# Five attention layers on one core: weights and context loaded before a branch, and the maxima of 16-head cross-attention split over two items

## The chip, the cores and the metric

The kernel runs on one core of a Trainium2 chip. The metric is the device time of one execution in microseconds (us). Before the change three runs took 2417.28, 2418.72 and 2425.54 us, a median of 2418.72.

A core has engines that run side by side, each through its own list of instructions, in order: PE (TensorE, matrix multiplication, and PEld, its loads of the stationary operand), DVE (VectorE), ACT (ScalarE), POOL (GpSimd) and SP (SyncE, here only the issuer of DMAs). An instruction that waits holds up all that stand behind it on its engine. Matrix results land in PSUM, from where DVE or ACT take them to SBUF ("evacuate" them); here PSUM is divided into a pool p1 of four buffers and a pool pb of two.

## The reference

Four sequences (batches) x of 1024 tokens by 256 channels, and a context of 77 rows by 256 for each batch, go through these layers, with residuals:

```python
# layer 0: pre-norm; self-attention with a mask, cross-attention, feed-forward
h = layernorm(x); x = x + mha16(h, h, h, mask)
h = layernorm(x); x = x + mha16(h, ctx, ctx)
h = layernorm(x); x = x + relu(h @ w1 + b1) @ w2
# layer 1: three times 4-head attention with relu on Q, K, V; first to ctx, then to itself
#   enc = norm(softmax(Q K' / 8, masked rows) V + q); enc += leaky_relu(enc @ Wff + bff)
# layer 2 (l2): 16-head cross-attention to ctx, out projection, residual, layernorm
# layer 3 (l3): 16-head cross-attention to ctx, no projection, residual, layernorm
```

All of it is in float32. The mask of these inputs lets the tokens of the first self-attention see only a few (at most 32) keys, all among the last ones. The kernel finds that out on the chip, and branches on it.

## The kernel before

*Items.* The work is cut into items, one for each batch and layer: four of the masked self-attention with few keys (SelfFew), four of layer 0's cross-attention (Cross16 with the layer named ca, whose feed-forward is part of the item's end), four of layer 1's first attention (Cross4), eight of its self-attention (Self4), four Cross16 of l2 and four Cross16 of l3. In time they take roughly 30 to 240 us (SelfFew), 240 to 605 (ca and its feed-forward), 605 to 1900 (layer 1), 1900 to 2180 (l2) and 2180 to 2417 (l3).

*Stages of an item.* An item has three lists of work. `start()` prepares it: norm, turning tokens to channels, queries, maxima. `attend()` yields units, 8 of them for Cross16: four groups of heads (g) for each half of the tokens (c = 0, 1; 512 tokens each). `end()` finishes it: projection, residual, norm, feed-forward. `Pipe.run` walks through the items' units, and at each unit a `Pump` (L84) issues steps between the unit's scores and its weighted sum. A pump draws on two lists: the first has `item.more()` and the `start()` of the next item, the second the `end()` of the item before. A step has a cost; the pump issues so many that the share of the costs done keeps up with the share of the units done, choosing the list that is further behind. A step's `lag` keeps its successor in the list back until that much cost has been issued, and a `test` keeps it back until something has happened. At the last unit everything left is issued. `until(test)` issues steps of the first list, without regard to shares, until the test holds: `attend()` calls it before the first unit of each half, where the half's shift must be there. This fixes the order on PE, which is issued as written; the order on DVE, ACT and POOL is made by a scheduler from the same program.

*A unit of Cross16.* `scores` (L335): the eight matmuls L346 and L352 make scores pb of four heads, with the shift added by the four of L352, and two exponentials on ACT (L356) make PT. `weighted` (L359): the matmuls L365 make po, evacuated to OT by ACT or DVE. A unit later `normal` (L372) transposes OT (L377) and divides by the sum (r, L380, and att, L382, on DVE).

*Maxima and shift.* So that the exponentials stay in range, each query's score is shifted by its maximum over the keys. `maxima(e, t)` (L265) makes all scores of eight heads for 128 tokens with two matmuls into two p1 buffers (pa, L270), and two DVE reductions take the maxima (mx, L275). For a half there are eight maxima (e = 0, 1 and four t). `shift(c)` (L296) follows: four DVE operations (L304 to L307) split the negated maxima into three bfloat16 parts (m), PE transposes them (pm, L310), and the result is evacuated to SH, which L352 adds. In `Cross16.start` (L213) the order is, for c = 0 and then c = 1: norm, two turns (L252), two queries (L260), eight maxima, shift. So both halves' maxima are issued in the attention of the item before. SelfFew does the same with its own maxima (L914, L921), four for each half.

*Norms.* At the end of an item of l2 and l3, `stats` and `norm` (L428, L432) run on DVE, with one small POOL operation between (pw, L1509): batch norm statistics (L1500, L1501), then L1547 and L1550, x with weight and bias of the norm. For l2 and l3 the next layer's turns read x as it is; where a layer has a norm in front (ca, feed-forward, SelfFew) a normalised copy xn is made in a buffer with the tag F, of which there is one.

*The beginning.* `branch` (L1915) loads the mask (raw, 1 MB of bytes, two DMAs issued by ACT) and x[0] (1 MB, SP). `mask_kind` (L1754) casts the mask to bfloat16 in eight pieces (mk, four buffers; L1766 on DVE, L1768 on ACT), sums its columns on PE (L1770), and DVE derives from the sums which kind of mask it is (kind). `orders` (L1815) prepares constants, `few_keys` (L1793) the valid keys, `first_norm` (L1877) the norm of x[0], `context` (L1862) loads the context per batch (cx, 77 rows, four DMAs issued by POOL into two buffers), transposes it (L1870) and sums it (ctx_sums, L1872). Then the engines read kind and branch. Behind the branch `l0_weights` (L1889) issues the self-attention's weights on SP (wk, wv, wq, wo; wk and wq share a buffer wqk), and two small loads on POOL (bvc and row, L1897 and L1899); x[1] and x[2] follow on SP, and x[3] later, in the place of a buffer that the beginning used. `LayerFew.steps` (L796) has a step `close`: DVE copies Q's and K's weights without their padding into a buffer named room (L812). Keys (pk, L877) and queries (pp, L867) of SelfFew read them there.

Of the kernel before, what the change touches and what calls it, by code (L numbers as in the profile page):

```python
# [83 lines left out]
class Pump:  # L84
# [32 lines left out]
    def until(self, test):  # L117
        while not test():
            self.take(0)


class Pipe:
# [26 lines left out]
    def run(self, items):  # L149
        pump = Pump(self, 1, items[0].start(), [])  # L150
        pump.until(lambda: items[0].halves >= 1)
        left = pump.lists[0]
        before = None
        for a, b in zip(items, items[1:]):
            b.prev = a
        for i, item in enumerate(items):
            last = i + 1 == len(items)
            first = left + ([] if last else items[i + 1].start())
            second = (before.end() if before else []) + (item.end() if last else [])
            left = []  # L160
            idle = item.idle()
            self.pump = pump = Pump(self, item.units + idle, item.more() + first, second)
            for _ in range(idle):
                self.unit()
            for scores in item.attend():
                self.unit(scores, item.cost)
            before = item
        while self.due:
            pump.n = 0
            self.unit()  # L170
        pump.n = pump.units - 1
        pump()


class Item:
# [5 lines left out]
    def more(self):  # L181

        return []

# [4 lines left out]
    def __init__(self, net, layer, b):  # L189
        self.net, self.l, self.b = net, layer, b  # L190
        self.halves, self.ended = 0, 0
        self.prev, self.later_half = None, True

    def room(self):
# [10 lines left out]
class Cross16(Item):  # L205
# [7 lines left out]
    def start(self):  # L213
# [23 lines left out]
        def norm(c):  # L237
            if l.norm is None:
                self.xn = x[:, 4 * c : 4 * c + 4, :]
                return  # L240
            mv, rstd = self.mv, self.rstd
            self.xn = net.tile("F", [P, 4, C], name="xn")
            for i in range(4):
                t = 4 * c + i
                nc.vector.tensor_scalar(
                    self.xn[:, i, :], x[:, t, :], mv[:, t, 0:1], rstd[:, t : t + 1], ALU.subtract, ALU.mult
                )

        def turn(c, cc):
            pt = net.p1.tile([P, 512], F32, tag="p1", name="pt")  # L250
            for i in range(4):
                nc.tensor.transpose(pt[:, ts(i, P)], self.xn[:, i, ts(cc, P)], net.ident)  # L252
            at = None if l.norm is None else COL_LN + 4 * (l.norm - 1) + cc
            g, be = (None, None) if at is None else (net.cols[:, at : at + 1], net.cols[:, at + 2 : at + 3])
            net.evac(self.hT[:, cc, ts(c, 512)], pt, g, be)

        def query(e, c):
# [22 lines left out]
        step(0, new, lag=8 * ln)  # L280
        for c in range(2):
            step(0, norm, c, lag=3 * ln)
            step(0.5, turn, c, 0)
            step(0.5, turn, c, 1, lag=2)
            if c == 0:
                step(0, new_q, test=self.room)
            for e in range(2):
                step(1.8, query, e, c)
            for e in range(2):
                for i in range(4):  # L290
                    step(0.55, maxima, e, 4 * c + i, lag=3 if (e, i) == (1, 3) else 0)
            step(0.3, self.shift, c)
            step(0, self.have_half)
        return steps

    def shift(self, c):  # L296

        net, h = self.net, H16
        nc = net.nc
# [6 lines left out]
        nc.vector.tensor_copy(parts[1], left)  # L306
        nc.vector.tensor_tensor(parts[2], left, parts[1], ALU.subtract)  # L307
        pm = net.p1.tile([P, 512], BF16, tag="p1", name="pm")
        for i in range(4):
            nc.tensor.transpose(pm[:, ts(i, P)], m3[:, i, :], net.identb)  # L310
        net.evac(self.sh[:, c, :], pm)
# [219 lines left out]
class Feed:  # L531
# [15 lines left out]
    def steps(self, b):  # L547
# [10 lines left out]
        def norm(c):  # L558
            s["xn"] = net.tile("F", [P, 4, C], name="xn")
            for i in range(4):  # L560
                t = 4 * c + i
                nc.vector.tensor_scalar(
                    s["xn"][:, i, :], x[:, t, :], s["mv"][:, t, 0:1], s["rstd"][:, t : t + 1], ALU.subtract, ALU.mult
                )

        def turn(c, cc):
            pt = net.p1.tile([P, 512], F32, tag="p1", name="pt")
            for i in range(4):
                nc.tensor.transpose(pt[:, ts(i, P)], s["xn"][:, i, ts(cc, P)], net.ident)
            at = COL_LN + 8 + cc  # L570
            net.evac(s["hT"][:, cc, ts(c, 512)], pt, net.cols[:, at : at + 1], net.cols[:, at + 2 : at + 3])

        def hidden(q, f):
# [31 lines left out]
        for c in range(2):  # L605
            step(0, norm, c, lag=3)
            step(0.5, turn, c, 0)
# [26 lines left out]
class Self16(Cross16):  # L634
# [8 lines left out]
    def start(self):  # L643
# [19 lines left out]
        def norm(c):  # L663
            self.xn = net.tile("F", [P, 4, C], name="xn")
            net.normal(self.xn, x, self.mv, self.rstd, c)

        def turn(c, cc):
            net.turn_normal(self.hT, self.xn, 1, c, cc)

        def query(g, c):  # L670
# [51 lines left out]
        for c in self.cs:  # L722
            if b:
                step(0, norm, c, lag=3)
                step(0.5, turn, c, 0)
# [60 lines left out]
class LayerFew:  # L786
# [9 lines left out]
    def steps(self):  # L796
# [5 lines left out]
        def close():  # L802
# [7 lines left out]
            for kind in ("wk", "wq"):  # L810
# [3 lines left out]
                    self.w[kind].rearrange("p cc (h r) -> p (cc h) r", r=h.slot)[:, :, 0 : h.dh],  # L814
                )
            self.pick = part(256, BF16).rearrange("p (g n) -> p g n", g=G)
            net.nc.vector.tensor_copy(
# [10 lines left out]
class SelfFew(Cross16):  # L828
# [5 lines left out]
    def start(self):  # L834
# [22 lines left out]
        def norm(c):  # L857
            self.xn = net.tile("F", [P, 4, C], name="xn")
            net.normal(self.xn, x, self.mv, self.rstd, c)

        def turn(c, cc):
            net.turn_normal(self.hT, self.xn, 1, c, cc)

        def query(e, c):
# [59 lines left out]
        for c in self.cs:  # L924
            if b:
                step(0, norm, c, lag=3)
                step(0.5, turn, c, 0)
# [7 lines left out]
            for t in range(4 * c, 4 * c + 4):  # L935
                step(0.9, maxima, t, lag=3 if t % 4 == 3 else 0)
            step(0.3, self.shift, c)
# [514 lines left out]
class Net:  # L1452
    def __init__(self, ctx, tc, t):
        self.ctx, self.tc, self.nc, self.t = ctx, tc, tc.nc, t
        self.flip = 0

    def evac(self, out, src, scale=None, bias=None):
# [127 lines left out]
    def load_attention(self, name, has_wo, tag):  # L1587
        nc, t = self.nc, self.t
        got = {}
        kinds = [("wk", 512), ("wv", C), ("wq", 512)] + ([("wo", C)] if has_wo else [])  # L1590
        both = self.work.tile([P, 2, NC, 512], F32, tag=tag, name="wqk", bufs=self.TAGS[tag][1])
        for kind, width in kinds:
            w = both[:, int(kind == "wq")] if width == 512 else self.wpool.tile(
                [P, NC, width], F32, tag=kind, name=kind, bufs=2 if kind == "wo" else 1
# [159 lines left out]
    def mask_kind(self, pool, raw):  # L1754
# [8 lines left out]
        for i in range(NT):  # L1763
            m = pool.tile([P, S], BF16, tag="mk", name="mk", bufs=4)
            if i % 3 == 0:
                nc.vector.tensor_copy(m, raw[:, i, :])  # L1766
            else:
# [93 lines left out]

    def context(self):  # L1862

        nc = self.nc
        for b in range(NB):
            cx = self.small.tile([SC, C], F32, tag="cx", name="cx", bufs=2)
            nc.gpsimd.dma_start(out=cx, in_=self.t["ctx"][b])
            pt = self.p1.tile([P, NC, P], F32, tag="p1", name="pt")
            for cc in range(NC):
                nc.tensor.transpose(pt[:, cc, 0:SC], cx[:, ts(cc, P)], self.ident[:SC, :SC])  # L1870
            self.evac(self.ctxT[:, :, ts(b, SC)], pt[:, :, 0:SC])
            nc.vector.tensor_reduce(self.ctx_sums[:, b : b + 1], cx, AX.X, ALU.add)  # L1872

# [15 lines left out]
    def l0_weights(self, few):  # L1889
# [3 lines left out]
        nc, h = self.nc, H16  # L1893
        w = self.load_attention("sa", True, "B" if few else "E")
        rows = self.t["rows"][ROW["sa"], :]
# [19 lines left out]
    def branch(self, out):  # L1915
        nc, tc = self.nc, self.tc
        with tc.tile_pool(name="begin", bufs=1) as pool:
            raw = pool.tile([P, NT, S], U8, tag="rawk", name="rawk")
            for i in range(2):
# [3 lines left out]
                )  # L1923
            self.load_x(0)
            self.orders(pool)
            kind = self.mask_kind(pool, raw)
            self.few_keys(pool)
            self.first = self.first_norm(pool)
            self.context()

# [11 lines left out]
        with branch.Else():  # L1942
            with tc.If(asked(1) > 0) as general:
                with tc.tile_pool(name="work_g", bufs=1) as self.work:
                    w = self.l0_weights(False)
                    for b in range(1, NB):
                        self.load_x(b)
# [5 lines left out]
    def few_layer(self):  # L1953
        w = self.l0_weights(True)
        for b in range(1, NB - 1):
            self.load_x(b)
        return [(SelfFew, LayerFew(self, w))]

    def short_layer(self):
        w = self.l0_weights(False)  # L1960
        for b in range(1, NB - 1):
            self.load_x(b)
        return [(Self16, Layer16Self(self, w))]
# [191 lines left out]
```

## Time and profile before

| | |
|---|---|
| time of the three runs | 2417.28, 2418.72, 2425.54 us |
| time of the profiled execution | 2419.14 us |
| its span | 2417.3 us |
| mean granted TensorE clock | 0.951 of full speed |
| PE busy | 2196.4 us (91%) |
| DVE busy | 1582.1 us (65%) |
| ACT busy | 928.9 us (38%) |
| POOL busy | 382.3 us (16%) |
| maxima, L270 on PE | 167.2 us busy, 768 matmuls |
| maxima, L275 on DVE | 156.0 us busy, 384 operations |
| scores of Cross16, L346 | 114.5 us busy, 768 matmuls |
| weighted sums of Cross16, L365 | 136.8 us busy, 768 matmuls |
| HBM | 17.41 MB read, 4.19 MB written |

The profile is one execution. The page divides the span into 40 equal slices; each digit is an engine's busy share in tenths, and the line PEclk the clock that the TensorE was granted. In lines of the timeline the columns are the start in us, the time in us, the engine, the line of the kernel, the operation, the result and its operands, their shapes, how many such instructions in a row; in square brackets the idle time of the engine just before, and what ended it. In lines of the waits: an engine and the line that waited, what for, total us, number of times, the longest.

### The profile page before, as it was taken

How to read it: one execution, taken by the hardware profiler on the slowest of the kernel's cores; microseconds unless marked ns; L12 is line 12 of the kernel's file. 1: busy time of each engine (PE TensorE's matmuls, PEld its weight loads, DVE VectorE, ACT ScalarE, POOL GpSimd, SP SyncE). 2: the span in 40 equal slices, each digit the busy share in tenths (PEclk: the TensorE clock that was granted, in tenths of full speed). 3: DMA queues.
4: the chain of work that ended last, by engine and by line, in shares of the span. 5: the costliest groups of instructions: out<-in, count | busy, mean ns of one | idle time of the engine just before them, and what ended most of it. 6: DMA issues, size and time to landing. Idle time of an engine off the chain costs nothing. (4 is left out here: it accounts for less than half of the span.)

```text
span 2417.3 us, 31250 instructions
## 1 busy us (share of the span) xinstructions
PE 2196.4 (91%) x11035; PEld 1226.0 (51%) x11035; DVE 1582.1 (65%) x3170; ACT 928.9 (38%) x1828; POOL 382.3 (16%) x652
## 2 busy tenths in 40 slices
PE   4899999999999979999998999999999899898886
PEld 2556546666768645545443545444444444444331
DVE  5566655444233666888889688878887655655665
ACT  1222342222332545544444445444443343333333
POOL 2000000000000000333333233333232100000000
PEclk8999999999989989999999999999999898998888
DMA  4000010000000001677667576666785300000000
GB/s 128 18 1 16 5 35 1 1 7 5 7 5 3 1 5 34 149 160 151 144 144 159 120 149 146 148 148 146 154 156 111 70 5 1 5 1 1 27 18 28
DMA packets 148550, 158.01 MB, mean 65 GB/s; under 512 B 51489, under 2 KB 130658, under 8 KB 148386
## 3 DMA queue, kind: packets, MB, share of 16 engines
q1 hardware_dynamic: 121842, 85.31, 16.6%
q0 software_dynamic: 25488, 69.56, 12.8%
q8 instruction: 91, 1.49, 0.3%
q10 hardware_dynamic: 1056, 1.05, 0.1%
q14 instruction: 73, 0.60, 0.1%
HBM read 17.41 MB, written 4.19 MB: 9 GB/s over the span
## 5 line engine op out<-in xcount | busy, mean ns | idle before, releaser
L1247 ACT ACTIVATE PR<-ss,nm 128x1024 f32<-128x1024 f32 x256 | 284.8, 1114 | 381.1 <-DVE nm L1241 294.4
L1259 DVE STREAM_TRANSPOSE PR<-PR 128x2048 f32<-128x2048 f32 x128 | 295.8, 2311 | 130.4 <-ACT PR L1247 115.5
L1266 POOL DMA_DIRECT2D PT<-PR x512 | 279.8, 554 | 591.9 <-PE ss L1230 227.9
L1230 PE MATMUL ss<-QK 64*128 64x512 f32 x1024 | 322.9, 630 | 26.3 <-ACT PR L1247 26.1
L1241 DVE TENSOR_REDUCE nm<-ss 128x1 f32<-128x1024 f32 x256 | 299.7, 1210 | 20.0 <-PE ss L1230 19.9
L1302 PE MATMUL po<-PT,V 128*64 128x256 f32 x2048 | 252.4, 389 | 2.3 <-DVE mx L275 2.2
L356 ACT ACTIVATE PT<-pb 77x1024 f32<-77x1024 f32 x192 | 185.4, 1016 | 178.4 <-PE pb L352 178.4
L275 DVE TENSOR_REDUCE mx<-pa 128x4 f32<-128x308 f32 x384 | 156.0, 469 | 71.2 <-PE pa L270 70.6
L1230 PEld LDWEIGHTS ss<-QK 64*128 64x128 f32 x1024 | 112.7, 188 | 172.0 <-ACT PR L1247 94.5
L270 PE MATMUL pa<-KA,QT 64*128 64x308 f32 x768 | 167.2, 490 | 30.2 <-DVE mx L275 29.8
L1302 PEld LDWEIGHTS po<-PT,V 128*64 128x64 f32 x2048 | 137.1, 138 | 106.1 <-issue 46.3
L365 PE MATMUL po<-PT,Vc 77*32 77x512 f32 x768 | 136.8, 652 | 18.5 <-ACT PT L356 9.6
L270 PEld LDWEIGHTS pa<-KA,QT 64*128 64x128 f32 x768 | 101.5, 197 | 97.3 <-DVE mx L275 45.4
L1509 POOL TENSOR_TENSOR pw<-va,minus_half 128x4 f32<-128x4 f32 (+1 forms) x28 | 38.0, 1358 | 619.7 <-DVE va L1507 542.0
L1469 ACT COPY OT<-po 128x512 f32<-128x512 f32 x57 | 33.4, 587 | 231.2 <-PE po L365 217.5
L346 PE MATMUL pb<-QT,KA 32*77 32x512 f32 x768 | 114.5, 668 | 0.0
L595 PE MATMUL pp<-w,hid 128*128 128x256 f32 x512 | 114.0, 381 | 0.0
L580 PE MATMUL pp<-hF,w 128*128 128x256 f32 x512 | 113.2, 379 | 0.0
L595 PEld LDWEIGHTS pp<-w,hid 128*128 128x128 f32 x512 | 96.5, 190 | 15.9 <-DVE mx L275 2.5
L580 PEld LDWEIGHTS pp<-hF,w 128*128 128x128 f32 x512 | 97.1, 190 | 14.6 <-issue 1.3
L1500 DVE BATCH_NORM_STATS2 st<-x 128x6 f32<-128x256 f32 x256 | 97.7, 405 | 5.6 <-DMA x<-in_x 4.4
L1373 PE MATMUL pp<-wo,hE 128*128 128x256 f32 x384 | 96.4, 393 | 1.6 <-ACT hE L1476 1.5
(257 smaller groups left out, 3147.3 us busy)
## 6 DMA issues: line engine op xcount, KB each, us to landing
PT<-PR SPq DMA_DIRECT2D x512, 128.0 KB, 5.5
PT<-PR POOLq DMA_DIRECT2D x512, 128.0 KB, 4.6
x<-in_x SPq DMA_DIRECT2D x4, 1024.0 KB
out<-x SPq DMA_DIRECT2D x8, 512.0 KB, 2.9
w<-in_ff_w SPq DMA_DIRECT2D x2, 1024.0 KB
gb<-in_norms POOLq DMA_DIRECT2D x5, 256.0 KB, 7.2
wk<-in_l_wk SPq DMA_DIRECT2D x10, 128.0 KB
wv<-in_l_wv SPq DMA_DIRECT2D x5, 256.0 KB, 3.5
```

The source lines that it names most:

```text
L270: nc.tensor.matmul(pas[i], self.qt[rows, e, ts(t, P)], self.ka[rows, e, :, :], start=True, stop=True)
L275: nc.vector.tensor_reduce(out, pas[i].rearrange("p (j s) k -> p j s k", s=2), AX.X, ALU.max, negate=True)
L356: nc.scalar.activation(pt[:, 2 * i : 2 * i + 2, :], pbs[i][:SC], AF.Exp, scale=self.l.scale)
L365: nc.tensor.matmul(po[ts(j, h.slot), :], l.v[:, self.b, col : col + h.vw], pt[:, j, :], start=True, stop=True)
L580: nc.tensor.matmul(pp[:, i, :], self.w1[:, cc, ts(f + i, P)], s["hT"][:, cc, ts(q, 2 * P)], start=cc == 0, stop=cc == NC - 1)
L595: nc.tensor.matmul(pp[:, u, :], s["a"][:, f, ts(u, P)], self.w2[:, f, :], start=f == 0, stop=f == NF - 1)
L1230: nc.tensor.matmul(ss[h][:, k, :], self.qk[p][rows, 0, ts(t, P)], self.qk[p][rows, 1, ts(k, 512)], start=True, stop=True,)
L1241: nc.vector.tensor_reduce(self.nm[:, t, at], s2, AX.X, ALU.max, negate=True)
L1247: nc.scalar.activation(out, s2, AF.Exp, bias=self.nm[:, t, at], accum_out=self.sums[:, t, at])
L1259: nc.vector.transpose(part, part)
L1266: (nc.sync, nc.gpsimd)[a % 2].dma_start(out=pt[ts(c, 32), :, :, a].rearrange("p t h k j -> p (t h) (k j)"), in_=pr[ts(a, 32), :, :, ts(c, ...
L1302: nc.tensor.matmul(po[64 * h : 64 * h + 64], self.v[:, k, 64 * (2 * p + h) : 64 * (2 * p + h) + 64], pts[:, :, h, :, k, :] if net.blocks e ...
```

## The change

*The beginning.* Q's and K's weights of the self-attention are loaded on SP ahead of the branch, into the buffer of x[2], which is still free there; the context comes in one SP DMA behind them, and x[1] behind that. The casts of the mask get eight buffers, and the norm of x[0] is issued behind the last of the casts on DVE (`issue_after`). The sums of the context are one reduction for all batches. `load_x(2)` moves into `close`, behind the copies that read the weights.

```diff
@@ branch @@
             self.load_x(0)
+            self.early = self.x[NB - 2].rearrange("p t c -> p (t c)").rearrange("p (e cc o) -> e p cc o", e=2, cc=NC)
+            for w, kind in zip(self.early, ("wk", "wq")):
+                nc.sync.dma_start(out=w, in_=self.t["sa_" + kind].rearrange("(cc p) o -> p cc o", p=P))
+            cx = pool.tile([SC, NB, C], F32, tag="cx", name="cx")
+            nc.sync.dma_start(out=cx, in_=self.t["ctx"].rearrange("b s c -> s b c"))
+            self.load_x(1)
             self.orders(pool)
             kind = self.mask_kind(pool, raw)
             self.few_keys(pool)
-            self.first = self.first_norm(pool)
-            self.context()
+            with tc.issue_after(self.turned_mask.ins):
+                self.first = self.first_norm(pool)
+            self.context(cx)
@@ mask_kind @@
-            m = pool.tile([P, S], BF16, tag="mk", name="mk", bufs=4)
+            m = pool.tile([P, S], BF16, tag="mk", name="mk", bufs=NT)
             if i % 3 == 0:
-                nc.vector.tensor_copy(m, raw[:, i, :])
+                self.turned_mask = nc.vector.tensor_copy(m, raw[:, i, :])
@@ context @@
-    def context(self):
+    def context(self, cx):
         nc = self.nc
         for b in range(NB):
-            cx = self.small.tile([SC, C], F32, tag="cx", name="cx", bufs=2)
-            nc.gpsimd.dma_start(out=cx, in_=self.t["ctx"][b])
...
-                nc.tensor.transpose(pt[:, cc, 0:SC], cx[:, ts(cc, P)], self.ident[:SC, :SC])
+                nc.tensor.transpose(pt[:, cc, 0:SC], cx[:, b, ts(cc, P)], self.ident[:SC, :SC])
             self.evac(self.ctxT[:, :, ts(b, SC)], pt[:, :, 0:SC])
-            nc.vector.tensor_reduce(self.ctx_sums[:, b : b + 1], cx, AX.X, ALU.add)
+        nc.vector.tensor_reduce(self.ctx_sums, cx, AX.X, ALU.add)
@@ few_layer @@
         w = self.l0_weights(True)
-        for b in range(1, NB - 1):
-            self.load_x(b)
@@ LayerFew.steps, close, behind the copies of L812 @@
+            net.load_x(NB - 2)
```

*The 16-head attention.* `Cross16.start` issues the turns and queries of both halves and the maxima and shift of the first half; those of the second half go into `self.rest`, which the item gives its own attention through `more()`. The four DVE operations that split the maxima become a step `thirds` of their own, ahead of `shift`, in SelfFew too.

```diff
@@ Item @@
     def more(self):
-        return []
+        return self.rest
@@ Cross16.start @@
-        for c in range(2):
-            step(0, norm, c, lag=3 * ln)
+        def turns(c):
+            step(0, norm, c, lag=3 * ln, test=net.not_held if ln else None)
             step(0.5, turn, c, 0)
             step(0.5, turn, c, 1, lag=2)
-            if c == 0:
-                step(0, new_q, test=self.room)
-            for e in range(2):
-                step(1.8, query, e, c)
+
+        turns(0)
+        step(0, new_q, test=self.room)
+        for e in range(2):
+            step(1.8, query, e, 0)
+        turns(1)
+        self.rest = Steps()
+        for c in range(2):
+            step = (steps, self.rest)[c].add
             for e in range(2):
                 for i in range(4):
-                    step(0.55, maxima, e, 4 * c + i, lag=3 if (e, i) == (1, 3) else 0)
+                    step(0.55, maxima, e, 4 * c + i, lag=0.5)
+                if c == 0 and e == 0:
+                    step(1.8, query, 0, 1)
+            step(0, self.thirds, c, lag=2)
+            if c == 0:
+                step(1.8, query, 1, 1)
             step(0.3, self.shift, c)
             step(0, self.have_half)
@@ SelfFew.start @@
-                step(0.9, maxima, t, lag=3 if t % 4 == 3 else 0)
+                step(0.9, maxima, t)
+            step(0, self.thirds, c, lag=3)
             step(0.3, self.shift, c)
```

*What keeps the buffer F in order.* A flag `held` is set where a normalised copy xn is made, and cleared where its second turn is issued; a norm step has the test that it isn't set. `until` takes a step of the second list where the first's next step is held back by its test.

```diff
     def until(self, test):
         while not test():
-            self.take(0)
+            first = self.lists[0][0]
+            self.take(0 if first.test is None or first.test() or not self.lists[1] else 1)
```

## What the change is predicted to do

> **What bounds the kernel now.** I read the page's slices first, then TensorE's waits over the last stage, its timeline around each wait, and the windows for the granted clock.
>
> ```profile
> PE   4899999999999979999998999999999899898886
> PEclk8999999999989989999999999999999898998888
> ```
>
> A slice is 60.4 us. TensorE is the bound nearly everywhere; it falls short in slice 1 (the beginning) and, with its clock, in several slices from the 32nd on (t = 1873: the end of the last self-attention, then the 16-head layers l2 and l3). The change works in both places, and in the 16-head cross-attention of layer 0 (t = 246 to 605). The beginning, on TensorE:
>
> ```profile
> 32.02 0.49 PE L1870 MATMUL pt<-ident,cx 77*128 77x77 f32 x2 [1.70 <-DMA cx<-in_ctx]
> 38.15 1.89 PE L877 MATMUL pk<-x,room 128*128 128x32 f32 x8 [5.64 <-DVE room L812]
> 41.56 5.57 PE L867 MATMUL pp<-x,room 128*128 128x512 f32 x8 [1.53 <-DVE ks L891]
> 55.35 0.40 PE L310 MATMUL pm<-identb,m 128*128 128x128 bf16 x4 [3.90 <-DVE m L307]
> ```
>
> The keys start at 38.15, because VectorE copies the weights late (L812 at 37.63 and 41.00), because it sat in order behind this:
>
> ```profile
> 37.02 0.69 DVE L405 TENSOR_TENSOR x<-x,row 128x512 f32<-128x512 f32 x1 [3.62 <-DMA row<-in_rows]
> ```
>
> The last stage (2000 to 2410), engine, line, releaser, total us, times, longest:
>
> ```profile
> PE pa L270 <- DVE mx L275: 19.1, 6, 5.0
> PE pm L310 <- DVE m L307: 13.0, 6, 3.7
> PE po L365 <- DVE hT L1465: 7.3, 2, 3.7
> PE po L365 <- ACT PT L356: 6.3, 12, 0.6
> ```
>
> Maxima and the shift built from them wait for VectorE. A stall is often followed by a slow clock; columns are the window, busy PE, PEld, DVE, ACT, POOL, then the clock:
>
> ```profile
> 2020.00:2030.00 10.00, 6.69 (x40) 3.78 (x32) 8.45 (x23) 2.52 (x3) 2.63 (x3) 0.76 0.00 0
> 2030.00:2040.00 10.00, 8.30 (x45) 4.12 (x45) 4.04 (x11) 2.73 (x4) 0.00 (x0) 0.56 0.01 2
> 2302.00:2304.00 2.00, 1.99 (x12) 1.26 (x16) 0.88 (x3) 0.00 (x0) 0.00 (x0) 0.50 0.00 0
> ```
>
> A cold us of TensorE counts (1 − clock) as lost. Summed over 10-us windows, 2000 to 2400 loses 36.7 us so. One episode costs about 3 us: after 2302 the clock is 0.50 for some 6 us, and eight pb take 2.00 for 1.10, eight po 1.94 for 1.06.
>
> **The beginning.** Q and K weights (two of 512 KB), the context (0.3 MB) and x[1] (1 MB) now follow x[0] on SP. x[0] and the mask had landed by 9.3, at 344 to 370 GB/s; 2.3 MB more at that rate take 6.6 us, so all is there by about 16. Their SP issues (0.4 to 0.7 us each) delay nothing, SP is idle then. POOL loses four context issues of 0.55 us, two of which had waited 9.51 us for a buffer until 27.47; bvc and row, behind them, go out near 24 instead of 29.1 and 29.9, and row, which took 7.1 us to land (29.9 to 37.0), is there at 31. With eight mask buffers ScalarE's wait of 8.28 us goes, and the second half of the mask is cast before the statistics: TensorE's mask sums end near 18 instead of 20.4. But VectorE must still do xn after POOL's 1.67 us of pw, so the verdict on the mask (kind, 23.98) moves only 1.0 to 1.5 us forward.
>
> After it, VectorE has some 5 us of work before the branch (24.04 to 28 without its waits for cx), then L817 and cneg (0.43 and 0.41), then the two copies at 0.42, now ahead of the additions of row. No context (31.91) and no row (37.02) stands before them. So the keys start near 29.5, 8.7 earlier; the queries after pk 1.9, L888 0.41, L891 0.21 at 32.0 instead of 41.56. From there the order to pm is the same. I take −9.5. Bounds: −1.3 (the verdict alone, if another wait takes its place) and −11.5.
>
> What this rests on: x[2] may be loaded only after the copies, since the weights lie in it. Its issue moves from 29.85 to about 29.3, alone with wv and wo on the queue; 1 MB at 300 GB/s and some 2 us lands it near 35. VectorE reaches x[2]'s statistics near 36, in order, with the maxima of the first attention behind them: each us of lateness there costs TensorE one us. The ca weights wait behind x[2] on SP, and are first needed at 225 (L501).
>
> **The 16-head attention.** The matmuls are the same ones. What moves, for each of 12 items: eight maxima (0.72 to 0.79 us TensorE, 0.80 to 0.94 VectorE each) and the second shift leave the previous item's attention and run in the first four units of the item's own. An attention unit without any filling work takes 4.35 us (2370.05, 2374.36, 2378.73: pb, exponentials, po), of which TensorE works 3.1; so one maxima in such a unit is free. The steps between units are placed by shares of cost, and the changed order shows what that gives: layer 2's items have 3, 2, 1, 1 maxima in units 0 to 3 and one more forced; l3's one each and four forced; those of ca two or three forced. Forced work is followed directly by the thirds and pm: VectorE needs its last mx (0.40), 1.1 us of thirds (2300.86 to 2301.95) and what lies ahead, so a stall of 2.0 to 2.7 us stays in every item. Queued behind it on TensorE are the next unit's pb and the po of the last one; ScalarE's exponentials wait for those.
>
> 1. *ca, four items.* Gone: pm 5.7 us (3 times 1.89) and pa 3.1 us. New: three forced blocks at 2.3 = 7; units 4 to 6 have no filling now in any item, 12 empty units at 1.26 = 15 where some 7 were lost before: +8. Cold: 3 us, one episode for three stalls. Sum −8.8 + 7 + 8 + 3 = **+9** (+4 to +17).
> 2. *End of the last self-attention (1870 to 1900).* It prepared the first l2 item: stalls of 1.95, 1.80, 3.10 and a po of 2.2, and 4.9 cold. It loses eight maxima, 6.6 us of TensorE at a place where VectorE is 80% busy. I count the 6.6 and a quarter of the stalls and cold: **−10** (−6.6 to −17).
> 3. *2000 to 2280, four items.* Stalls of pa and pm are 7.8, 4.3, 7.5 and 8.7 by item, 28.3 in all; cold by 10-us windows 24.9. After: a pm stall of 2.0, one backlog of pa behind statistics and norm (nearest rows: its smaller waits, 2.41 to 2.82; I take 2.5), one cold episode, 7.5 an item. 30 − 53 = **−23** (−15 with two cold episodes an item and a smaller backlog, −39 with none).
> 4. *l3, two filled items.* One took 58.07 (2282.18 to 2340.25), with 3.66 for hT, 1.89 for pm and 5.9 cold. hT's wait goes, since the norm block no longer meets the turns there; the forced pm costs 2.7 and 3, a backlog 1.25 and its cold 2: 8.9 for 11.4: −2.5 each, **−5** (0 to −11).
> 5. *The last item.* It has no filling, so it pays: eight maxima that were another item's, four in idle units, four forced (0.82 each), 2.7 for pm, 3 cold: **+9** (+6 to +12).
>
> Sum: −9.5 + 9 − 10 − 23 − 5 + 9 = −29.5. The profiled execution's time is 2419.1 (span 2417.3 and 1.8 around it), 0.4 above the median 2418.7. So 2389 against the median.
>
> The weighed place is the cold episode. In this trace these two rows had equal stalls:
>
> ```profile
> 257.99 0.40 PE L310 MATMUL pm<-identb,m 128*128 128x128 bf16 x4 [1.89 <-DVE m L307]
> 2302.01 0.61 PE L310 MATMUL pm<-identb,m 128*128 128x128 bf16 x4 [1.89 <-DVE m L307]
> ```
>
> The clock stayed 1.00 after the first and was 0.50 after the second. So a stall of 1.89 is sometimes enough, and I charge one episode to most forced blocks late in the kernel and one in three in ca. [...]
>
> **Rivals.** (a) *The 16-head part comes to nothing.* Each of twelve forced blocks stalls 2.3 and is cold for 3: 64 us, about what stalls and cold of points 1 to 4 cost now. Then only the beginning is left: 2409. For it: the stall of m is as long as the chain mx, thirds, whatever runs ahead. Against it: the pa waits, the larger part, have VectorE's norm blocks as cause, and fewer maxima meet them.
>
> (b) *More goes.* Thirds as a step of their own, issued before the last query, hide pm in l2 items, and clock episodes go with the stalls: points 3 and 4 at their lower bounds, −39 and −11, others as above: 2367.
>
> (c) *The beginning gains little*, since x[2] comes late and holds VectorE, or the verdict still sets the keys: −1.5 for −9.5: 2397.
>
> (d) *Slower.* A maxima inside a unit is not free: its mx stands on VectorE behind copies of po, r and att, with four PSUM buffers shared with po, and delays that unit's po and so the next pb. Priced at one mx pair, 0.85, in 48 units (12 items by 4): 41 us, so −29.5 + 41 = +11: 2430. It decides from 0.62 us a unit on. For it: l2's units are full, without idle to absorb; 2.56 us of L1550 in one run can stand ahead. Against: before, the same maxima stood in the same kind of units.
>
> **How the numbers follow.** Forecast 0.45, (a) 0.18, (b) 0.17, (c) 0.07, (d) 0.13. No change means within 0.3%, 7.3 us, about what a measurement of this kernel can tell. The forecast, (b), nearly all of (c) and about two thirds of (a) lie under 2411.5: faster 0.79. The rest of (a) and a little of (c) and (d): same 0.09; slower 0.12. The range leaves out the lower half of (b) and most of (d): 2366 to 2420. The likeliest alone: 2376 to 2402, where its own points' bounds partly cancel.
>
> **What would show it.** Keys (L877's like) near 29.5 and the first pm near 45.5; row and cx no longer in VectorE's waits; the second mask cast right behind the first. In the last stage: total waits of pa under 12 us and of pm near 2 to 2.7 in each item; hT gone; clock sums of 2000 to 2400 near 25. If pm stalls grew past 3 or clocks fell to 0.5 in ca, (a) or (d) holds. If VectorE waits for x[2] at 36, (c). The forecast is wrong if units 0 to 3 lengthen beyond 4.35 us where nothing but one maxima fills them.

## The result and the profile after

Six runs of the changed kernel have a median of 2401.91 us (2396.79 to 2409.13), six of the kernel before beside them 2419.16 us. The ratio is 0.9929 with a 95% interval of 0.9913 to 0.9944: 0.7% faster, 17 us, where 30 were forecast. The profiled execution took 2396.79 us, 22.3 less than the profiled one of before; it is the fastest of the six, and its granted clock, 0.958, the highest (the run of 2407.01 us had 0.951).

The page's slices of the kernel after:

```profile
PE   6899999999898979999999899999999899999996
PEclk8999989989998998999999999999999899999988
```

The first slice went from 4 to 6 and the last ones from 8 to 9, but in the slices 6 to 13 (299 to 778 us, layer 0's cross-attention and feed-forward) the clock now shows three 8s where before there was one. The beginning in TensorE's timeline:

```profile
28.37 1.88 PE L908 MATMUL pk<-x,room 128*128 128x32 f32 x8 [1.10 <-issue]
30.06 5.71 PE L898 MATMUL pp<-x,room 128*128 128x512 f32 x8
42.77 0.40 PE L331 MATMUL pm<-identb,m 128*128 128x128 bf16 x4 [2.69 <-DVE mv L1537]
```

Keys, queries and the first shift start 9.8, 11.5 and 12.6 us earlier. The waits of the last stage (2000 to 2410), same columns as before:

```profile
PE pm L331 <- DVE m L323: 11.1, 6, 2.1
PE pa L276 <- DVE mx L281: 8.9, 7, 2.6
PE po L386 <- ACT PT L377: 3.2, 6, 0.6
```

The waits for mx fell from 19.1 to 8.9, hT's 7.3 are gone, those for m are nearly as long as they were.

Where the time went, cut at the same matmuls in both traces (the first pm, each item's first L352 or L373, the feed-forward's last matmul). "Idle" is time without a matmul, "cold" half of the matmul time in stretches with the clock at 0.5 (an upper bound of what the clock costs, since a matmul's row can hold a wait):

| section | before: us (idle, cold) | after: us (idle, cold) |
|---|---|---|
| to the first pm | 55.3 (32.3, 4.5) | 42.8 (17.9, 5.8) |
| SelfFew | 220.1 (20.8, 3.4) | 210.4 (17.2, 3.4) |
| ca and feed-forward | 514.2 (22.2, 11.2) | 548.4 (33.5, 25.9) |
| layer 1 | 1114.8 (75.5, 34.7) | 1091.0 (66.7, 22.3) |
| l2, first item | 64.5 (2.4, 0) | 77.5 (9.6, 8.8) |
| next four items | 280.1 (33.7, 28.3) | 255.5 (17.7, 5.9) |
| l3, two filled items | 116.2 (12.6, 12.2) | 111.5 (5.8, 11.0) |
| last item, to the last matmul | 35.2 (4.7, 0.7) | 41.1 (5.7, 0) |

SelfFew is shorter by eight maxima that now count for ca. Taken together, SelfFew and ca lose 24.5 us, more than the beginning gains. In layer 1, most of whose order on TensorE is the same, one trace has slow stretches of the clock that the other hasn't; 12 of its 24 us are cold. Part of the gain there is luck: in the eleven other kernels below that split maxima the section takes 1093 to 1105 us, for 1091.0 here.

The loss in ca, at the second of its items:

```profile
340.23 2.53 PE L276 MATMUL pa<-KA,QT 64*128 64x308 f32 x12
345.67 0.61 PE L331 MATMUL pm<-identb,m 128*128 128x128 bf16 x4 [2.90 <-DVE mv L1537]
346.20 2.00 PE L367 MATMUL pb<-QT,KA 32*77 32x512 f32 x8
349.79 2.83 PE L386 MATMUL po<-PT,Vc 77*32 77x512 f32 x8
352.55 2.00 PE L367 MATMUL pb<-QT,KA 32*77 32x512 f32 x8
356.08 2.83 PE L386 MATMUL po<-PT,Vc 77*32 77x512 f32 x8
```

Three forced maxima, a stall of 2.90 for the thirds, then two units in which eight pb take 2.00 instead of 1.10 and eight po 2.83. The stall is longer than the 1.1 us of thirds: TensorE's last maxima end at 342.76, their reductions on VectorE 1.09 later, and VectorE has statistics of the feed-forward's norm ahead of the thirds and between them, which so take until 345.61:

```profile
343.01 0.84 DVE L281 TENSOR_REDUCE mx<-pa 128x4 f32<-128x308 f32 x2
...
344.18 0.22 DVE L320 CAST m<-mx 128x64 bf16<-128x64 f32 x1
...
344.57 0.42 DVE L1536 BATCH_NORM_STATS2 st<-x 128x6 f32<-128x256 f32 x1
...
345.33 0.28 DVE L323 TENSOR_TENSOR m<-rest,m 128x64 bf16<-128x64 f32 x1
```

### The profile page after: what moved, and what is told of

Its sections match the earlier page's. It is cut to its first block, busy times and chain, and to the rows that moved or that the text cites. A ratio compares the mean times of both kernels' runs of the same rounds, so it can differ in the third digit from the quotient of the medians.

```text
span 2394.9 us, 31195 instructions
## 1 busy us (share of the span) xinstructions
PE 2204.3 (92%) x11035; PEld 1204.8 (50%) x11035; DVE 1582.6 (66%) x3167; ACT 930.2 (39%) x1828; POOL 380.4 (16%) x648
## 3 DMA queue, kind: packets, MB, share of 16 engines
q1 hardware_dynamic: 122161, 85.63, 17.2%
q0 software_dynamic: 25296, 69.24, 13.1%
## 5 line engine op out<-in xcount | busy, mean ns | idle before, releaser
L1291 DVE STREAM_TRANSPOSE PR<-PR 128x2048 f32<-128x2048 f32 x128 | 295.8, 2311 | 128.9 <-ACT PR L1279 114.3
L281 DVE TENSOR_REDUCE mx<-pa 128x4 f32<-128x308 f32 x384 | 161.4, 470 | 83.7 <-PE pa L276 82.5
L276 PE MATMUL pa<-KA,QT 64*128 64x308 f32 x768 | 169.1, 486 | 14.0 <-DVE mx L281 12.8
L276 PEld LDWEIGHTS pa<-KA,QT 64*128 64x128 f32 x768 | 84.3, 193 | 99.1 <-issue 37.0
L619 PEld LDWEIGHTS pp<-w,hid 128*128 128x128 f32 x512 | 97.0, 190 | 16.5 <-issue 2.2
L266 PE MATMUL pp<-hT,wq 128*128 128x512 f32 x192 | 98.0, 646 | 5.5 <-ACT hT L1507 5.0
```

Source lines behind the costliest of these rows:

```text
L276: nc.tensor.matmul(pas[i], self.qt[rows, e, ts(t, P)], self.ka[rows, e, :, :], start=True, stop=True)
L281: nc.vector.tensor_reduce(out, pas[i].rearrange("p (j s) k -> p j s k", s=2), AX.X, ALU.max, negate=True)
L619: nc.tensor.matmul(pp[:, u, :], s["a"][:, f, ts(u, P)], self.w2[:, f, :], start=f == 0, stop=f == NF - 1)
L1291: nc.vector.transpose(part, part)
```

## The experiments

Each was timed in at least three rounds beside the kernel before; ratios are to that kernel.

**Each half alone.** One kernel has the change to the beginning alone (the first diff under "The change"), the other all the rest.

> The changed beginning alone, with the 16-head attention as before. Theory (the parts add up): the first pm comes 12.6 us earlier, as in the changed kernel's profile (42.77 for 55.35), and nothing later takes it back: 2419 - 12 = 2407. Rival (a wait of the first self-attention, behind x[2] for instance, eats it): 2414 to 2419, with the first ca unit less than 5 us earlier than before.

2402.19 us, ratio 0.9922 (0.9905 to 0.994).

> The split maxima alone, with the beginning as before. Theory: the changed kernel's gain of 17 less the beginning's 12 is left, about 2414, made of a loss of some 24 us from 275 to 801 (layer 0's cross-attention and feed-forward) and gains behind 1783. Rival (the attention part is a wash, and the rest is the clock's chance): 2419 to 2424, with the same sections but other signs.

2419.88 us, ratio 0.9976 (0.9958 to 0.9994).

The beginning alone is as fast as the whole change. Its first pm is at 43.45, and SelfFew and ca take 222.6 and 516.4 us, so nothing takes the gain back. It is even 5 us faster than expected: the first pm accounts for 11.9 us, and in this profile layer 1, whose order is unchanged, is 9 us shorter, most of it cold. The granted clock was 0.952 to 0.954 in its four runs and 0.945 to 0.951 in the thirteen of the kernel before; why it is higher stays open. The attention part alone is worth 0.24%, hardly more than nothing, which is the rival's time, but the sections are the theory's: SelfFew and ca together 765 us for 734 of before, and layer 1, l2 and l3 shorter, as in the changed kernel. The parts add up only just within their intervals (0.78 + 0.24 for 0.71%).

**What in the beginning.** The weights' or the context's part is undone.

```diff
-        w = self.load_attention("sa", True, None if few else "E")
+        w = self.load_attention("sa", True, "B" if few else "E")
...
-            self.early = self.x[NB - 2].rearrange("p t c -> p (t c)").rearrange("p (e cc o) -> e p cc o", e=2, cc=NC)
-            for w, kind in zip(self.early, ("wk", "wq")):
-                nc.sync.dma_start(out=w, in_=self.t["sa_" + kind].rearrange("(cc p) o -> p cc o", p=P))
```

> The changed kernel, but Q's and K's weights are loaded behind the branch as before, into their own buffer; context, mask and x[1] stay changed. Theory (that buffer lies where the beginning's tiles lay, so the load can only start once these are done, 27.90 before, not with the branch at 22.3): wk is issued at 26 to 27, both weights are there at 32 to 33, the keys start near 33 instead of 28.4, and the kernel is 4 to 5 slower than the changed one: 2406. Rival (the load goes out with the branch and lands in time): keys at 28.4 to 30, 2400 to 2403.

2410.79 us, ratio 0.9968 (0.9944 to 0.9992). Its queue and TensorE:

```profile
29.57 0.37 SPq L1637 DMA_DIRECT2D wqk<-in_sa_wk  x1
```

```profile
33.98 1.89 PE L908 MATMUL pk<-x,room 128*128 128x32 f32 x8 [4.54 <-issue]
39.61 6.14 PE L898 MATMUL pp<-x,room 128*128 128x512 f32 x7 [3.75 <-DVE room L839]
```

The load goes out at 29.57, not with the branch (the changed kernel's first load behind it, wv, went at 22.30), so the theory's direction holds; it missed the size. The keys are 5.6 late, the queries 9.6, the first pm (53.48) 10.7: VectorE copies K's weights at 33.4, but Q's only at 39.04, behind an xn that waits 1.45 for POOL. Not all of it is the load's. VectorE's order changed too; the sums of the context now stand ahead of the constants and of the third cast of the mask:

```profile
11.32 1.22 DVE L1911 TENSOR_REDUCE ctx_sums<-cx 77x4 f32<-77x1024 f32 x1 [4.97 <-DMA cx<-in_ctx]
```

That cast starts at 13.87 for 9.32, and kind is there at 23.83 for 21.35, so some 2.5 us of the lateness stand ahead of the branch and come from that order, not from the place of the load. That the buffer is what holds the load is argued from the code and from the queue's waits, which name the last readers of the beginning's tiles (xn, 2.4 us, and the transposes of the context, 2.2); it wasn't tried by itself.

For the context, `context` is put back as in the kernel before:

```diff
-            cx = pool.tile([SC, NB, C], F32, tag="cx", name="cx")
-            nc.sync.dma_start(out=cx, in_=self.t["ctx"].rearrange("b s c -> s b c"))
...
+            cx = self.small.tile([SC, C], F32, tag="cx", name="cx", bufs=2)
+            nc.gpsimd.dma_start(out=cx, in_=self.t["ctx"][b])
```

> The changed kernel, but with the context in four POOL transfers through two buffers, each summed by itself, as before; weights and mask stay changed. Theory (the last two transfers wait for PE's transposes of the first two, and VectorE waits for them in order ahead of the copies): VectorE's last ctx_sums ends near 31, keys start near 33 instead of 28.4, first pm near 47; 2406. Rival (the context is hidden once weights are early): keys at 28.4 to 30, 2400 to 2403.

2404.80 us, ratio 0.9944 (0.9924 to 0.9964), not to be told from the changed kernel's. In the trace ctx_sums ends at 29.4, keys start at 30.70 and the first pm at 45.42, 2.7 late, about half of what was expected; 1.0 of it is kind's (22.32). So the early weights are worth most of the 12.6 us, some 8 without the part ahead of the branch, and the context 2 to 3.

**Where the attention part loses.** First, ca as far as possible as before, then the changed split with another spreading of the second half's maxima.

```diff
-            step = (steps, self.rest)[c].add
+            step = (steps, self.rest if l.norm is None else steps)[c].add
```

> The changed kernel, but in layer 0's cross-attention all sixteen maxima stay in the previous item's attention. Theory (the forced shift in mid-attention, the cold clock after it and the empty units 4 to 6 make the loss there): the section of ca and its feed-forward falls from 548 us (253 to 801) to 530 or less, and the kernel to 2384 +- 6. Rival (the loss comes from the new order of turns and norms or from the clock's chance): the section stays above 540 and the kernel within 2396 to 2406.

2384.16 us, ratio 0.985 (0.9831 to 0.987); the section of ca takes 523 us, and SelfFew, which has the eight maxima back, 218.7 for 210.4. So the split costs 18 us in ca, and gains as much behind it (2402 with the beginning alone, 2384 with it and the split in l2 and l3); by the profiles half of that gain lies in layer 1 and half in l2 and l3.

```diff
-                    step(0.55, maxima, e, 4 * c + i, lag=0.5)
+                    step(0.55, maxima, e, 4 * c + i, lag=0.5 * (c == 0))
```

> The changed kernel, but the second half's maxima are issued without a lag between them, so that they are done in units 0 and 1 and no shift is forced in front of unit 4 (except in the last item). Theory (the forced shift costs some 2 us of idle TensorE and a cold clock of 1.5 to 8 us in each item): pm's waits for m in mid-attention go, 10 items by 2 to 3 us: 2402 - 25 = 2377. Rival (VectorE is the limit there): the stall turns into waits of pa for mx in unit 0, where up to five maxima stand in a row, and the time stays at 2396 to 2406.

2346.37 us, ratio 0.9692 (0.9676 to 0.9709): over four times the gain of the whole change, from one number, and 31 us better than expected. The second item of ca:

```profile
321.77 2.52 PE L276 MATMUL pa<-KA,QT 64*128 64x308 f32 x12
...
327.98 0.39 PE L331 MATMUL pm<-identb,m 128*128 128x128 bf16 x4
328.97 1.23 PE L386 MATMUL po<-PT,Vc 77*32 77x512 f32 x8 [0.17 <-DVE SH L1501]
```

The last maxima end at 324.3, other work lies between them and pm at 327.98, which waits for nothing, and the clock stays full. The second and third items of ca take 116.2 and 116.1 us for 131.3 and 128.9; of the 27.9 us gained, 11.9 are idle and 16.5 cold. The rival's waits of pa for mx are there (13.1 us from 1892 on, for 10.9), but small beside that.

The next two kernels use this order in ca alone, and in ca and l2.

```diff
+                    step(0.55, maxima, e, 4 * c + i, lag=0.5 * (c == 0 or l.norm is None))
```

> The changed kernel, with rest_lag0's order (second half's maxima without lag) in layer 0's cross-attention alone; l2 and l3 as in the changed kernel. Theory (the loss of the split sits in ca's forced shifts): the section from the first ca unit to the feed-forward's end falls by 35, as between the changed kernel (548) and rest_lag0 (513), and the kernel to 2367, 2358 to 2376. Rival (rest_lag0's gain is l2's): 2385 to 2400.

2370.18 us, ratio 0.9788 (0.9761 to 0.9815); SelfFew's end to the feed-forward's end 513 us. As expected.

```diff
+                    step(0.55, maxima, e, 4 * c + i, lag=0.5 * (c == 0 or l.out is not None))
```

> As rest_lag0 in ca and l2, but l3's second half keeps the changed kernel's lag of 0.5 (one maxima in each of units 0 to 3 and four forced). Theory (in l3 five maxima in a row meet VectorE's norm block of the item before and wait 2 to 4 us for it, more than the forced shift costs): l3's three items and the last take 153 as in the changed kernel for 158 in rest_lag0, the rest stays: 2341, 2334 to 2350. Rival (the forced shift is the worse one in l3 too): 2350 to 2362.

2349.62 us, ratio 0.9717 (0.9686 to 0.9748): not better than rest_lag0. l3's next two items take 53.0 and 52.1 for 58.1 and 54.9, the last 47.3 for 45.3: 152 together, as the theory had it. But l3's first item, which it left as it was, takes 65.7 for 59.9 and gives the gain back.

**Stall or clock.** In the next two kernels TensorE transposes the identity 16 times in front of a shift, into the shift's own buffer, and the shift overwrites it.

```diff
+        for _ in range(4):
+            for i in range(4):
+                nc.tensor.transpose(pm[:, ts(i, P)], net.identb, net.identb)
         for i in range(4):
             nc.tensor.transpose(pm[:, ts(i, P)], net.m3[c][:, i, :], net.identb)
```

> The changed kernel with 16 extra transposes of the identity on TensorE in front of each shift's four (their result is overwritten; some 1.2 us of useless work each time, placed where TensorE waits for m). Theory (a stall of about 2 us costs twice, by itself and by the half clock that follows when it leaves too little work in one 3.4 us window): the clock's loss in the sections 253 to 801 and 1892 to 2378, 26 us each, falls below 10 each, and the kernel to 2372 +- 10, with more matmuls than before. Rival (the cold clock comes from elsewhere, or the extra work only takes the idle's place): 2398 to 2412.

2396.99 us, ratio 0.9913 (0.9882 to 0.9943): the same as the changed kernel. Cold fell from 26 to 20 us in ca and from 26 to 11 behind 1892, and idle by 17 in all, but the useless work at all 32 shifts, most of which were not late, cost as much. Neither theory's number came.

```diff
+        for i in range(16 if self.rest and c else 0):
+            nc.tensor.transpose(pm[:, ts(i % 4, P)], net.identb, net.identb)
```

> The changed kernel, with the 16 extra transposes in front of the twelve forced shifts alone, where TensorE stalls 2 to 3 us for m. Theory (the half clock after a forced shift is decided by how much work lies in the window of the stall): the stalls themselves stay as long, the clock's loss in 253 to 801 and 1892 to 2378 falls from 26 and 26 us to under 15 and 12, without the 20 us that the extra work cost in warm at shifts that had no stall: 2382, 2374 to 2394. Rival (the clock falls anyway): 2397 to 2408.

2384.96 us, ratio 0.9858 (0.9827 to 0.9888), outside the changed kernel's interval: with 192 useless instructions more it is 17 us faster, as the theory had it. The place shown above, now:

```profile
341.56 1.07 PE L331 MATMUL pm<-identb 128*128 128x128 bf16 x16
344.53 0.43 PE L333 MATMUL pm<-identb,m 128*128 128x128 bf16 x4 [1.91 <-DVE mv L1539]
344.89 2.00 PE L369 MATMUL pb<-QT,KA 32*77 32x512 f32 x8
...
350.38 1.10 PE L369 MATMUL pb<-QT,KA 32*77 32x512 f32 x8
```

The real transposes wait for m as before, 2.9 us behind the last maxima; but the idle stretch is 1.91. The eight pb right behind still take 2.00, those of the next unit are back at 1.10. Busy times by windows of 4 us; the granted clock is the third number from the right. First the changed kernel, then this one:

```profile
344.00:348.00 4.00, 2.33 (x15) 0.89 (x16) 3.90 (x22) 0.59 (x1) 1.65 (x1) 0.60 0.94 330
348.00:352.00 4.00, 3.89 (x20) 1.09 (x12) 2.31 (x6) 1.93 (x2) 1.64 (x1) 0.50 0.00 0
352.00:356.00 4.00, 4.00 (x18) 1.27 (x16) 1.46 (x4) 0.99 (x2) 0.00 (x0) 0.50 0.00 0
```

```profile
344.00:348.00 4.00, 3.47 (x20) 1.49 (x20) 2.77 (x15) 1.18 (x2) 2.14 (x2) 0.60 0.70 233
348.00:352.00 4.00, 3.55 (x22) 0.65 (x20) 3.41 (x9) 1.62 (x3) 0.52 (x1) 0.98 0.00 0
352.00:356.00 4.00, 3.58 (x25) 1.14 (x26) 1.04 (x3) 2.23 (x3) 0.00 (x0) 1.00 0.00 0
```

The clock recovers after one slow window of 3.4 us where it had stayed down for five. This one place proves nothing: weights_late, without the transposes, recovers there after one window too. What carries the reading is the time, with four runs of 2378.16 to 2391.14, all below the six of the changed kernel, and the sum: over both sections the cold loss is 12.8 and 6.9 us, for 25.9 and 25.7. Since the real transposes come no earlier, the 17 us are the clock's.

**A spread that missed.** The maxima go 3, 3, 2 into units 0 to 2, the last item's too (a step of cost 9 without work at the end of its list).

```diff
+                    step(0.55, maxima, e, 4 * c + i, lag=0.5 if c == 0 or (e, i) in ((0, 2), (1, 1)) else 0)
+        if l.out is not None and b == NB - 1:
+            self.rest.add(9, lambda: None)
```

> As rest_lag0, but the second half's maxima go 3, 3, 2 into units 0 to 2 in place of 5, 3, and the last item does the same, so that no shift at all is forced. Theory (five maxima in a row leave TensorE waiting for VectorE's reductions; 13.1 us of pa waits and 5.1 of po behind SH in rest_lag0 from 1892 on): l3's items 58.1, 54.9 and 45.3 fall to about 50, 50 and 39, less some 6 in ca, whose units 4 to 6 are empty again: 2337, 2328 to 2346. Rival (VectorE's total work in the units is the limit): l3's items stay and the kernel is at 2346 to 2356.

2380.41 us, ratio 0.9858 (0.9826 to 0.989), against 2337 expected: wrong, and by the rival's number too. No shift is forced (in ca's fourth item pm still waits 1.74), but l3's items still take 58.8 and 55.1. TensorE and VectorE at the start of one:

```profile
2202.52 1.31 PE L276 MATMUL pa<-KA,QT 64*128 64x308 f32 x8
2206.10 1.77 PE L276 MATMUL pa<-KA,QT 64*128 64x308 f32 x4 [2.27 <-DVE mx L281]
```

```profile
2203.46 1.28 DVE L1588 SCALAR_TENSOR_TENSOR x<-x,pw,gb 128x256 f32<-128x256 f32 x3 [0.90 <-POOL pw L1547]
...
2205.57 1.62 DVE L281 TENSOR_REDUCE mx<-pa 128x4 f32<-128x308 f32 x4
```

The first maxima are issued at 2202.5 and reduced from 2205.57 on: the norm of the item before stands ahead on VectorE, in a wait of 0.90 for POOL. With two p1 buffers for each maxima, the third one waits (2.27 us), however many follow. The other losses against rest_lag0 are 10 us in ca's second and third items, whose units 4 to 6 have no filling again, 7 in l2's first item, and 14 in ca's fourth with its feed-forward, of which 13 are cold. Why the clock is so much worse there stays open.

**The best of it.** rest_lag0's order, except in l3's last three items, which keep the lag of 0.5 and get the 16 transposes.

```diff
+                    step(0.55, maxima, e, 4 * c + i, lag=0.5 * (c == 0 or l.out is not None and b > 0))
+        for i in range(16 if c and self.l.out is not None and self.b > 0 else 0):
+            nc.tensor.transpose(pm[:, ts(i % 4, P)], net.identb, net.identb)
```

> rest_lag0's order in ca, l2 and the first item of l3; the changed kernel's order in l3's other three items, whose forced shifts get the 16 extra transposes. Theory (every stall that stays is kept warm, every other is gone): l3's first item takes 60 as in rest_lag0 (66 in lag0_ca_l2), its next two 52, the last 41 (45 in rest_lag0): 2346 - 6 - 3 - 4 = 2333, 2328 to 2342. Rival (l3's differences are the clock's chance): 2343 to 2352, like rest_lag0.

2338.95 us (2336.53 to 2343.65), ratio 0.9656 (0.964 to 0.9673), 3.4% faster than the kernel before. Its slices:

```profile
PE   6899999999989979999999899999999999999996
PEclk8999999999999989999999999999999999999998
```

l3's items take 59.9, 56.5, 52.1 and 42.8 for 60, 52, 52 and 41 expected; between the first slice and the last the 9s of the clock now run through but for one slice. The time is within the range expected, and below the rival's.

## Why the prediction was right, and where it was wrong

The sign and the range held; the cause of the gain is not quite the forecast's. By its own points, from the profiled pair:

- *The beginning*, −9.5: measured −12.6. The mechanism was right; keys came at 28.37 for 29.5 and, the queries being ready at once behind them, the first pm at 42.77 for 45.5. The verdict (kind) came 2.5 earlier, for 1.0 to 1.5. x[2]'s late load held nothing; x[3]'s held VectorE for 2.33 at 56.9, and TensorE behind it for 0.8. By the medians the beginning alone is worth 17 to 20, more than its first pm shows.
- *1, SelfFew and ca*, +9: measured +24.5. This is the term that failed. Stalls and empty units were forecast at +6, idle grew by 7.7. Cold was put at 3, "one episode for three stalls", from three stalls of 1.89 that had left the clock alone; it grew by 14.7. The forced stalls were 2.9, 2.9 and 2.2 us, longer than those, and followed by units that are themselves little filled. It is not this execution's chance: attn_only, weights_late and context_late, with the same order in ca, have 37.1, 22.6 and 30.7 cold there. warm_forced shows the clock's part, lag0_ca both together.
- *2, end of the last self-attention*, −10: layer 1 gained 23.8, of it 12.4 cold, and the first l2 item lost 13.0. The sum of −10.8 fits the number, the picture doesn't: the shed maxima let TensorE run into a new wait, for the transposed probabilities' DMA, and the item's own maxima stalled instead:

```profile
1898.66 3.68 PE L1334 MATMUL po<-PT,V 128*64 128x256 f32 x16 [5.12 <-DMA PT<-PR]
1922.10 4.21 PE L276 MATMUL pa<-KA,QT 64*128 64x308 f32 x12 [2.03 <-DVE mx L281]
1928.01 0.61 PE L331 MATMUL pm<-identb,m 128*128 128x128 bf16 x4 [1.70 <-DVE m L323]
```

- *3, four items*, −23: measured −24.6. The direction of both terms was right, but the fit of the number is partly luck: idle fell from 33.7 to 17.7 and cold from 28.3 to 5.9, 38.4 together, while the same 1400 matmuls take 14 us longer in the rows (pa 5.4, po 5.3), as waits inside a row or because cold is an upper bound.
- *4, two l3 items*, −5: measured −4.7. Right in sum; the cold was 1.7 in one item and 9.3 in the other.
- *5, the last item*, +9: measured +5.9, since no cold followed its stall.

Sum −12.6 + 24.5 − 10.8 − 24.6 − 4.7 + 5.9 = −22.3. The medians give −17, for the profiled execution is the fastest of its six, and of that the beginning alone gives all: rival (a), that the 16-head part comes to nothing, describes the end of it better than the forecast, but not by its mechanism, since large gains and a large loss cancel. The range held because it was wide: the miss of 15.5 us in point 1 is half the forecast gain, and 3.1 us each at the beginning and in the last item, which came out better than forecast, made up for part of it. Rival (d)'s price showed in part: in the last item, where nothing but maxima fills the units, eight pb start at 2336.02, 2340.38, 2344.69 and 2349.77, so the units with one maxima take 4.36, 4.31 and 5.08 us for the 4.35 of an unfilled one.

The forecast's own sign against itself, a clock of 0.5 in ca, came. To weigh the clock by the trace was right in kind: in the four kernels with this order (the changed one, attn_only, weights_late, context_late) 44 stalls of pm in front of unit 4, 1.3 to 2.9 us each, make 91 us, and 21 of them were followed, within a window of 3.41 us, by a slow stretch; these stretches make 95 us of cold. In seven more the clock was already at 0.5. So in these four kernels the forced blocks cost about as much again in the clock as in the stalls. The slow stretches last 3.41, 6.83 or 10.24 us and so on (in the changed kernel's trace 10, 6 and 3 of its 25).

## What to carry to other kernels

When work is moved to another place, ask what must follow directly behind it there: here a step that is forced, with a chain on another engine between it and its data, cost its wait (91 us in 44 stalls) and, behind 21 of them, the clock as well (95 us). Read what a stall costs from the matmuls behind it (eight pb took 2.00 us for 1.10), not only from the waits. And, as rest_lag0 (2346.37 us) against rest_332 (2380.41) and the changed kernel (2401.91) shows, a lag or a share that spreads work evenly can be worse than a lump, if the lump leaves room before the deadline.

## What the runs showed of the hardware

In the clock records of these 14 traces the clock changes only on a fixed raster of 3.41 us. Of the full-speed windows of that raster (60 to 2330 us) with a matmul in less than 40% of their time, all 99 were followed by a slow one; with 40 to 50%, 79 of 144; 50 to 60%, 84 of 193; 60 to 70%, 31 of 196; 70 to 80%, 12 of 347; above that none of 7709. This fits a stall of 1.89 us that sometimes costs the clock and sometimes not: 1.52 us of 3.41 are left, 45%, if it falls wholly into one window. Once slow, the clock stayed slow behind all 96 windows with less than 80%, and still behind 184 of 477 with more than 90%; why behind those stays open. The six runs of the changed kernel span 12 us (2396.79 at a granted clock of 0.958, 2409.13 at 0.951), so gains of a few us can't be read from one profile.
